# Score products grouped by pass within a PSUM bank, and background VectorE work queued behind a slot's key scaling

## The chip, the cores and the metric

The kernel runs on one core of one Trainium2 chip. The metric is the device time of one execution in microseconds; where several executions were timed, the median is given.

## The reference, cut to what matters

A block of three parts adds to x (512 tokens in 8 groups of 64, width 512): a cross-attention part that also holds a self-attention, a sparse attention part, and a feed-forward part with ternary weights. Most of the time goes into the cross-attention over the context, which has 1601 rows for each of the 8 groups:

```python
kvx = jnp.einsum('bsi,oi->bso', cond, w_kv_x)
kx, vx = jnp.split(kvx, 2, axis=-1)
kx = _ln(kx.reshape(b, sc, g, d), kxln_w, kxln_b)      # g = 8 heads of d = 128
scores = jnp.einsum('bsghd,btgd->bghst', q, k) * scale
p = jax.nn.softmax(scores, axis=-1)
return jnp.einsum('bghst,btgd->bsghd', p, v)
```

The matrix products are wanted at float32 accuracy. The kernel therefore splits each operand into a high and a low part and adds three products: high by high, high by low, low by high.

## The kernel before, in words

**Foreground.** The 1601 context rows of a group are cut into 13 tiles of 128 (the last has 65). One loop runs over 208 slots, one for each tile of each of 16 `Cross` objects (8 groups by 2 halves of 4 heads each). A tile passes through these steps, each some slots after the one before:

- `keys` (L515 to L538): load, split into `cThi` and `cTlo` (ScalarE, GpSimd), twelve 512-wide matmuls into a PSUM bank `kx` (L528), squares on ScalarE (`sq`, L533), their sum on VectorE (`kxv`, L534), two small GpSimd operations that end with the reciprocal root `rqk` (L535, L173), and the scaling of the keys by it on VectorE (`kn`, L537). That last one releases the bank.
- `keys_t` (L540 to L553): four transposes of `kn` into another bank called `kx` (L219), then `kthi` on ScalarE (L550), the difference `kf` on VectorE (L552), and `ktlo` on ScalarE (L553).
- `scores` (L555 to L575), once per chunk of two tiles, or three for the last chunk. The scores of one head are 256 wide (322 in the last chunk). [...] Each head is three matmuls (L571 to L573) and one reduction on VectorE (L574), which copies the scores to the SBUF tile `S`, and whose accumulator is read out into the running maxima `cmx`.
- `probs_t`, `context`, `weigh`, 16 slots later: transposes of the exponentials `S` into a bank `pt` (L593), its split into `phi` and `plo`, and twelve 512-wide matmuls into four accumulator banks (L620 to L622).

**Banks.** After slot 15 the pool `pm` of three banks serves all of `kx` (both uses), `s`, `pt`, `xo` and `xt`. A bank's next matmul waits until the last reader of the bank's previous content is done.

**Background.** Projections, self-attention, the sparse attention and the making of ternary weights are Python generators in three streams, `bgA`, `bgB` and `bgC`. At the end of each slot the loop pumps some steps out of them (L1130 to L1137). For `bgB` the pump stands in `tc.issue_after(paced[0].ins)`, where `paced[0]` is the slot's load of context rows: instructions of the same engine as that load (the queue of SP) are queued behind it.

**Order.** The instructions are not queued in the order in which they are written. A scheduler orders each engine's queue when the program is built, using its own model of time; every engine then runs its queue strictly in that order. `tc.issue_after(x)` is a constraint for this scheduler: what the block adds on the engine of `x` stands behind `x` in that engine's queue. It adds no wait between engines.

Of the kernel before, what the change touches and what calls it, by code (L numbers as in the profile page):

```python
# [4 lines left out]

# [12 lines left out]
ALU = mybir.AluOpType  # L18
# [3 lines left out]
P = 128  # L22
# [4 lines left out]
D = 128  # L27
NH = 16
G = 8
HG = 4  # L30
# [7 lines left out]
NCH = len(CHUNKS)  # L38
# [19 lines left out]
def tile_perceiver(ctx: ExitStack, tc: tile.TileContext, t: dict):  # L58
    nc = tc.nc
    V, A, GP, PE = nc.vector, nc.scalar, nc.gpsimd, nc.tensor  # L60
# [16 lines left out]
    def nm(s):  # L77
        uid[0] += 1
        return f"{s}_{uid[0]}"

    def ctile(shape, dt, tag):
        return const.tile(shape, dt, tag=tag, name=tag)

    def sm(tag, k=1, dt=F32, bufs=None):
        kw = {} if bufs is None else {"bufs": bufs}
        return small.tile([P, k], dt, tag=tag, name=nm(tag), **kw)
# [5 lines left out]
    def mainp(tag="m"):  # L92
        return pm.tile([P, 512], F32, tag="m", name=nm(tag))

    def kxp(tag="kx"):


        if lane["late"] is not None:
            return lane["late"]
        return accp(tag) if lane["wide"] else mainp(tag)  # L100
# [35 lines left out]
    def v3(ap, g):  # L136
        return ap.rearrange("p (g k) -> p g k", g=g)
# [4 lines left out]
    class Late:  # L142
# [13 lines left out]
        ps = staticmethod(lambda tag="b": kxp())  # L156
# [68 lines left out]
    zeros = ctile([P, 1], F32, "zeros")  # L225
# [264 lines left out]
        return hi, lo  # L490

    paced = [None]

    class Cross:

# [19 lines left out]
        def keys(self, tt):  # L515

            t0, n = TT[tt]
            raw = mp.tile([P, NIC, P], F32, tag="raw", name=nm("cTr"), bufs=3)
            paced[0] = nc.sync.dma_start(raw[:, :, :n], t["ctxT"][self.b].rearrange("(c p) k -> p c k", p=P)[:, :, t0:t0 + n])
            chi = mp.tile([P, NIC, P], F32R, tag="cThi", name=nm("cThi"), bufs=2)  # L520
            clo = mp.tile([P, NIC, P], F32R, tag="cTlo", name=nm("cTlo"), bufs=2)
            A.copy(chi[:, :, :n], raw[:, :, :n])  # L522
            GP.tensor_tensor(clo[:, :, :n], raw[:, :, :n], chi[:, :, :n].bitcast(F32), ALU.subtract)  # L523
            ps = kxp()
            k = 0
            for st, mv in ((chi, self.wk[0]), (chi, self.wk[1]), (clo, self.wk[0])):
                for ic in range(NIC):
                    PE.matmul(ps[:n], lhsT=st[:, ic, :n], rhs=mv[:, ic, :], start=k == 0, stop=k == 11)  # L528
                    k += 1
            kn = mp.tile([P, 512], F32, tag="kn", name=nm("kn"), bufs=3)  # L530
            sq = mp.tile([P, 512], F32, tag="sq", name=nm("sq"), bufs=1)
            v = sm("kxv", HG)
            A.activation(sq[:n], ps[:n], AF.Square, scale=1.0 / math.sqrt(D))  # L533
            V.tensor_reduce(v[:n], v3(sq[:n], HG), AX.X, ALU.add)  # L534
            GP.tensor_scalar(v[:n], v[:n], EPS, None, ALU.add)  # L535
            r = rsqrt(v[:n], n, HG, "rqk")
            V.tensor_tensor(v3(kn[:n], HG), v3(ps[:n], HG), r.unsqueeze(2).to_broadcast([n, HG, D]), ALU.mult)  # L537
            self.kn[tt] = kn  # L538

        def keys_t(self, tt):  # L540
# [14 lines left out]
        def scores(self, ci):  # L555
            chunk = CHUNKS[ci]
            cw = sum(TT[tt][1] for tt in chunk)
            hi, lo = self.kt.pop(ci)
            N = cw + (cw & 1)
            if N > cw:  # L560
                GP.memset(hi[:, :, cw:N].bitcast(F32), 0.0)
                GP.memset(lo[:, :, cw:N].bitcast(F32), 0.0)
            sc = mp.tile([P, HG, KTW], F32, tag="S", name=nm("S"), bufs=7)
            self.S[ci] = sc
            per = 512 // N
            for g in range(HG):
                if g % per == 0:
                    bank = mainp("s")
                ps = bank[:, g % per * N:(g % per + 1) * N]
                q = slice(g * P, (g + 1) * P)  # L570
                PE.matmul(ps, lhsT=self.qhi[:, q], rhs=hi[:, g, :N], start=True, stop=False)  # L571
                PE.matmul(ps, lhsT=self.qhi[:, q], rhs=lo[:, g, :N], start=False, stop=False)
                PE.matmul(ps, lhsT=self.qlo[:, q], rhs=hi[:, g, :N], start=False, stop=True)  # L573
                V.tensor_tensor_reduce(sc[:, g, :cw], ps[:, :cw], zeros.to_broadcast([P, cw]), 1.0, -3.0e38,  # L574
                                       ALU.add, ALU.max, self.mx[:, g * NCH + ci:g * NCH + ci + 1])  # L575

        def maxima(self):
            self.nmx = sm("cnm", HG)
# [467 lines left out]
    bgB = Stream()  # L1046
# [4 lines left out]
    for g in range(NA + LAG + 3):  # L1051
        nA, kA = divmod(g, NT)
        if g < NA and kA == 0:
            h = work[nA].half
            if h not in wk:
                wk[h] = key_weights(h)
            work[nA].wk = wk[h]
        if g == LAG - 1:
            lane["wide"] = False
        if g == NA + 3:  # L1060
            lane["late"] = mainp("late")
        e = g - LAG + 1
        if 0 <= e < NA:
            nE, kE = divmod(e, NT)
            w = work[nE]
            w.context(kE)
            w.probs_t(kE)
            ci = CHUNK_OF[kE]
            if ci + 1 < NCH:

                with tc.issue_after(w.pin.ins):
                    w.exps(ci + 1, *((0, 2) if kE == CHUNKS[ci][0] else (2, 4)))
        if g < NA:
            work[nA].keys(kA)
        if g == 0:
            bgA.pump(ALL)
        if g == 2:
            bgA.add(norms(rest), projection("qx", range(4), rest), projection("qx", range(4, 8), range(NJ)),
                    projection("q", range(8), range(NJ)), projection("k", range(4), range(NJ)), projection("v", range(4), range(NJ)))
            bgA.add(*[self_attn(j) for j in range(NJ)])  # L1080
            bgA.add(attn_consts())
        if g == TERNARY_AT:
            bgB.add(ternary("ffn_w1", w1t), ternary("ffn_w2", w2t))
        if 0 <= g - 2 < NA:
            nS, kS = divmod(g - 2, NT)
            ci = CHUNK_OF[kS]
            w = work[nS]
            if kS == CHUNKS[ci][-1]:
                if ci == 0:
                    w.queries()  # L1090
                w.scores(ci)
                if ci == NCH - 1:
                    w.maxima()
                    w.exps(0, 0, 2)
        if 0 <= g - 3 < NA and (g - 3) % NT == NT - 1:
            work[(g - 3) // NT].exps(0, 2, 4)
        e = g - LAG
        if 1 <= e and e % NT == 0 and e // NT <= len(work):
            work[e // NT - 1].values()
        if 2 <= e and (e - 1) % NT == 0 and (e - 1) // NT <= len(work):  # L1100
            w = work[(e - 1) // NT - 1]
            key = (w.b // 2, w.half)
            j, odd = divmod(w.b, 2)
            split = w.half and j >= NJ - SPLIT
            if not odd:
                bgA.clear_front()
                if w.half:
                    bgA.pump(ALL)
                catq[key] = cat_tile("catx")
            w.cat(catq[key])  # L1110
            if key != (NJ - 1, 1):
                if not w.half:
                    if odd:
                        bgA.front.append(proj_part(j, 16, catq[key]))
                elif split or odd:
                    on = (odd * S, S) if split else (0, P)
                    bgA.add(finish(j, 24, catq[key], *on))
            elif not odd:
                bgC.add(proj_weights(24), finish(NJ - 1, 24, catq[key], 0, S, True, Late()))
            else:  # L1120
                bgA.add(finish(NJ - 1, 24, catq[key], S, S, True))
        if 0 <= e < NA:
            nE, kE = divmod(e, NT)
            work[nE].weigh(kE)
            if kE == NT - 1:
                work[nE].weighed()
        if 0 <= g - 1 < NA:
            nT, kT = divmod(g - 1, NT)
            work[nT].keys_t(kT)
        for bg, q in ((bgA, PACE[g >= LATER]), (bgC, PACE[1]), (bgB, TERNARY_PACE if g < NA + FFN_AT else 0)):  # L1130
            n = int((g + 1) * q) - int(g * q)
            if bg is bgB:

                with tc.issue_after(paced[0].ins):
                    bg.pump(n)
            else:
                bg.pump(n)  # L1137
        if g == NA + FFN_AT:
            bgB.pump(ALL)
            if NJ > 2:  # L1140
                bgB.add(ffn(list(range(NJ - 2)), 0))
                bgB.step()
# [74 lines left out]
```

## Time and profile before

| what | value |
|---|---|
| median of 3 runs | 2084.85 us (2074.91 to 2086.65) |
| the profiled execution | 2083.31 us |
| its span, first to last instruction | 2081.6 us |
| mean granted TensorE clock | 0.988 |
| TensorE matmuls busy | 1979.7 us, 10923 records |
| VectorE, ScalarE, GpSimd busy | 1390.4, 1304.4, 952.9 us |
| DMA | 257.34 MB, mean 124 GB/s |
| last score matmul starts | 1885.4 us |

A busy time of matmuls is not their work: the matmuls overlap, and their ends are modelled. In the timeline, 512-wide matmuls that follow each other without a wait start about 0.23 us apart, 256-wide ones 0.12 us, 128-wide ones 0.11 us, while the record of one lasts 0.39, 0.28 and 0.27 us. Idle time of TensorE is thus the time in which not even a tail of a record is left. In the list of waits each line gives the waiting instruction, what released it, the total in us, the number of times, and the longest.

### The profile page before, as it was taken

How to read it: one execution, taken by the hardware profiler on the slowest of the kernel's cores; microseconds unless marked ns; L12 is line 12 of the kernel's file. 1: busy time of each engine (PE TensorE's matmuls, PEld its weight loads, DVE VectorE, ACT ScalarE, POOL GpSimd, SP SyncE). 2: the span in 40 equal slices, each digit the busy share in tenths (PEclk: the TensorE clock that was granted, in tenths of full speed). 3: DMA queues.
4: the chain of work that ended last, by engine and by line, in shares of the span. 5: the costliest groups of instructions: out<-in, count | busy, mean ns of one | idle time of the engine just before them, and what ended most of it. 6: DMA issues, size and time to landing. Idle time of an engine off the chain costs nothing. (4 is left out here: it accounts for less than half of the span.)

```text
span 2081.6 us, 32709 instructions
## 1 busy us (share of the span) xinstructions
PE 1979.7 (95%) x10923; PEld 1633.8 (78%) x10923; DVE 1390.4 (67%) x3344; ACT 1304.4 (63%) x2787; POOL 952.9 (46%) x1018
## 2 busy tenths in 40 slices
PE   5889999999999899999999999999999999999998
PEld 4778878888778788887888888787878778877776
DVE  7876676576676775767777777675755665576665
ACT  5666757677666666665656656666556665566554
POOL 5454545454454444445444544444454445542232
PEclk9999999999999999999999999999999999999999
DMA  5443343444334444544544454432433223333325
GB/s 180 127 116 112 113 124 110 122 135 127 107 117 130 140 144 123 173 133 156 161 142 148 142 176 145 142 106 69 127 104 109 77 77 97 87 93 101 114 69 170
DMA packets 261817, 257.34 MB, mean 124 GB/s; under 512 B 25408, under 2 KB 186304, under 8 KB 261648
## 3 DMA queue, kind: packets, MB, share of 16 engines
q1 hardware_dynamic: 261648, 255.25, 41.1%
q8 instruction: 86, 1.41, 0.3%
q14 instruction: 83, 0.68, 0.1%
HBM read 231.33 MB, written 23.59 MB: 122 GB/s over the span
## 5 line engine op out<-in xcount | busy, mean ns | idle before, releaser
L523 POOL TENSOR_TENSOR cTlo<-cTr,cThi 128x512 fp32r<-128x512 f32 (+1 forms) x208 | 267.6, 1286 | 497.7 <-ACT cThi L522 352.5
L607 POOL TENSOR_TENSOR clo<-cr,chi 128x512 fp32r<-128x512 f32 (+1 forms) x208 | 277.2, 1333 | 292.8 <-ACT chi L606 273.3
L621 PE MATMUL acc<-plo,chi 128*128 128x512 f32 (+1 forms) x832 | 336.0, 405 | 1.5 <-DVE plo L597 1.5
L622 PE MATMUL acc<-phi,clo 128*128 128x512 f32 (+1 forms) x832 | 327.0, 395 | 0.0
L534 DVE TENSOR_REDUCE kxv<-sq 128x4 f32<-128x512 f32 (+1 forms) x208 | 141.9, 682 | 237.3 <-ACT sq L533 236.7
L620 PE MATMUL acc<-phi,chi 128*128 128x512 f32 (+1 forms) x832 | 254.5, 405 | 5.6 <-ACT phi L596 2.9
L528 PE MATMUL kx<-wkhi,cThi 128*128 128x512 f32 (+1 forms) x832 | 242.9, 413 | 13.0 <-DVE kf L552 4.0
L550 ACT ACTIVATE kthi<-kx,cols 128x512 fp32r<-128x512 f32 (+1 forms) x208 | 159.0, 764 | 145.6 <-PE kx L219 144.7
L606 ACT CAST chi<-cr 128x512 fp32r<-128x512 f32 (+1 forms) x208 | 128.4, 617 | 166.9 <-PE acc L621 117.1
L528 PE MATMUL kx<-wklo,cThi 128*128 128x512 f32 (+1 forms) x832 | 229.4, 398 | 0.0
L173 POOL TENSOR_TENSOR rqk<-kxv,mhalf 128x4 f32<-128x4 f32 (+1 forms) x208 | 219.0, 1053 | 17.2
L528 PE MATMUL kx<-wkhi,cTlo 128*128 128x512 f32 (+1 forms) x832 | 225.7, 393 | 0.0
L522 ACT CAST cThi<-cTr 128x512 fp32r<-128x512 f32 (+1 forms) x208 | 125.2, 602 | 126.8 <-PE kx L528 59.9
L574 DVE CUSTOM_DVE_ANT_0 S<-s,zeros 128x256 f32<-128x256 f32 (+1 forms) x384 | 157.1, 429 | 64.4 <-PE s L573 63.2
L584 ACT ACTIVATE S<-S,cnm 128x256 f32<-128x256 f32 (+1 forms) x384 | 196.4, 518 | 1.8 <-DVE cnm L579 1.8
L528 PEld LDWEIGHTS kx<-wklo,cThi 128*128 128x128 f32 (+1 forms) x832 | 155.8, 187 | 40.9 <-POOL wklo L489 0.5
L528 PEld LDWEIGHTS kx<-wkhi,cThi 128*128 128x128 f32 (+1 forms) x832 | 146.8, 188 | 50.1 <-DVE cmx L574 6.8
L620 PEld LDWEIGHTS acc<-phi,chi 128*128 128x128 f32 (+1 forms) x832 | 151.5, 189 | 42.8 <-ACT phi L596 5.8
L552 DVE SCALAR_TENSOR_TENSOR kf<-kx,cols,kthi 128x512 f32<-128x512 f32 (+1 forms) x208 | 150.8, 725 | 49.9 <-ACT kthi L550 49.0
L528 PEld LDWEIGHTS kx<-wkhi,cTlo 128*128 128x128 f32 (+1 forms) x832 | 153.9, 185 | 38.2
L537 DVE TENSOR_TENSOR kn<-kx,rqk 128x512 f32<-128x512 f32 (+1 forms) x208 | 142.5, 685 | 59.0 <-POOL rqk L173 57.9
L621 PEld LDWEIGHTS acc<-plo,chi 128*128 128x128 f32 (+1 forms) x832 | 157.0, 189 | 29.1 <-DVE plo L597 2.2
(320 smaller groups left out, 4120.2 us busy)
## 6 DMA issues: line engine op xcount, KB each, us to landing
cTr<-in_ctxT SPq DMA_DIRECT2D x192, 256.0 KB
cr<-in_ctx SPq DMA_DIRECT2D x192, 256.0 KB
ld<-in_wproj SPq DMA_DIRECT2D x128, 256.0 KB
wv<-in_wkv SPq DMA_DIRECT2D x64, 256.0 KB
tern<-in_ffn_w SPq DMA_DIRECT2D x64, 256.0 KB
wb<-w1t SPq DMA_DIRECT2D x24, 256.0 KB
wb<-w2t SPq DMA_DIRECT2D x24, 256.0 KB
ld<-lnTd SPq DMA_DIRECT2D x19, 256.0 KB
```

The lines of the kernel that those rows point to most:

```text
L173: GP.tensor_tensor(y[:n], v, mhalf[:n, :k], ALU.pow)
L523: GP.tensor_tensor(clo[:, :, :n], raw[:, :, :n], chi[:, :, :n].bitcast(F32), ALU.subtract)
L528: PE.matmul(ps[:n], lhsT=st[:, ic, :n], rhs=mv[:, ic, :], start=k == 0, stop=k == 11)
L537: V.tensor_tensor(v3(kn[:n], HG), v3(ps[:n], HG), r.unsqueeze(2).to_broadcast([n, HG, D]), ALU.mult)
L550: A.activation(hi[:, :, o], v3(pt, HG)[:, :, :n], AF.Identity, bias=hb["kx"], scale=hw["kx"])
L552: V.scalar_tensor_tensor(kf[:, :, :n], v3(pt, HG)[:, :, :n], hw["kx"], hi[:, :, o].bitcast(F32), ALU.mult, ALU.subtract)
L574: V.tensor_tensor_reduce(sc[:, g, :cw], ps[:, :cw], zeros.to_broadcast([P, cw]), 1.0, -3.0e38, ALU.add, ALU.max, self.mx[:, g * NCH + ci:g ...
L584: A.activation(self.S[ci][:, g, :cw], self.S[ci][:, g, :cw], AF.Exp, bias=self.nmx[:, g:g + 1], accum_out=self.su[:, g * NCH + ci:g * NCH ...
L607: GP.tensor_tensor(clo[:n], raw[:n], chi[:n].bitcast(F32), ALU.subtract)
L620: PE.matmul(self.U[ic], lhsT=chi[:n, s], rhs=phi[:n], start=tt == 0, stop=False)
L621: PE.matmul(self.U[ic], lhsT=chi[:n, s], rhs=plo[:n], start=False, stop=False)
L622: PE.matmul(self.U[ic], lhsT=clo[:n, s], rhs=phi[:n], start=False, stop=last)
```

## The change

Two things change. In `scores`, the matmuls of all heads in a bank are issued pass by pass: first high by high for each head, then low query by high key, and last high query by low key. Only the first matmul into the bank carries the start flag. The reductions of the bank's heads follow after all of its matmuls. In the main loop, all three background streams are pumped in `tc.issue_after(pin[0].ins)`, where `pin[0]` is the newest scaling of keys (`kn`), a VectorE instruction; `bgB` keeps its other constraint.

```diff
+    pin = [None]
...
-            V.tensor_tensor(v3(kn[:n], HG), v3(ps[:n], HG), r.unsqueeze(2).to_broadcast([n, HG, D]), ALU.mult)
+            pin[0] = V.tensor_tensor(v3(kn[:n], HG), v3(ps[:n], HG), r.unsqueeze(2).to_broadcast([n, HG, D]), ALU.mult)
...
             per = 512 // N
-            for g in range(HG):
-                if g % per == 0:
-                    bank = mainp("s")
-                ps = bank[:, g % per * N:(g % per + 1) * N]
-                q = slice(g * P, (g + 1) * P)
-                PE.matmul(ps, lhsT=self.qhi[:, q], rhs=hi[:, g, :N], start=True, stop=False)
-                PE.matmul(ps, lhsT=self.qhi[:, q], rhs=lo[:, g, :N], start=False, stop=False)
-                PE.matmul(ps, lhsT=self.qlo[:, q], rhs=hi[:, g, :N], start=False, stop=True)
-                V.tensor_tensor_reduce(sc[:, g, :cw], ps[:, :cw], zeros.to_broadcast([P, cw]), 1.0, -3.0e38,
-                                       ALU.add, ALU.max, self.mx[:, g * NCH + ci:g * NCH + ci + 1])
+            for g0 in range(0, HG, per):
+                bank = mainp("s")
+                gs = range(g0, g0 + per)
+
+                for k, (a, x) in enumerate(((self.qhi, hi), (self.qlo, hi), (self.qhi, lo))):
+                    for i, g in enumerate(gs):
+                        PE.matmul(bank[:, i * N:(i + 1) * N], lhsT=a[:, g * P:(g + 1) * P], rhs=x[:, g, :N],
+                                  start=k == 0 and i == 0, stop=k == 2, skip_group_check=True)
+                for i, g in enumerate(gs):
+                    ps = bank[:, i * N:(i + 1) * N]
+                    V.tensor_tensor_reduce(sc[:, g, :cw], ps[:, :cw], zeros.to_broadcast([P, cw]), 1.0, -3.0e38,
+                                           ALU.add, ALU.max, self.mx[:, g * NCH + ci:g * NCH + ci + 1])
...
-            if bg is bgB:
-
-                with tc.issue_after(paced[0].ins):
-                    bg.pump(n)
-            else:
+
+            with tc.issue_after(pin[0].ins), tc.issue_after(paced[0].ins) if bg is bgB else nullcontext():
                 bg.pump(n)
```

More of the change, by code (lines that the diff above doesn't have):

```diff
@@ L2 @@
 from collections import deque
-from contextlib import ExitStack
+from contextlib import ExitStack, nullcontext
 from types import SimpleNamespace
```

## The prediction

> **What bounds the kernel now.** I read the page first: TensorE is busy in 95% of the span and in eight or nine tenths of nearly every slice, VectorE in 67%.
>
> ```profile
> span 2081.6 us, 32709 instructions
> ...
> PE 1979.7 (95%) x10923; PEld 1633.8 (78%) x10923; DVE 1390.4 (67%) x3344; ACT 1304.4 (63%) x2787; POOL 952.9 (46%) x1018
> ...
> PE   5889999999999899999999999999999999999998
> ```
>
> So TensorE's queue sets the end. An edit pays only if it shortens TensorE's work, which it doesn't (same matmuls, same sizes), or its waits. The list of TensorE's waits is therefore the second view:
>
> ```profile
> PE pt L593 <- DVE cmx L574: 14.0, 16, 1.9
> ...
> PE kx L219 <- DVE kn L537: 10.4, 13, 3.6
> PE kx L219 <- DVE cmx L574: 6.3, 13, 1.5
> PE s L571 <- DVE cmx L574: 6.1, 10, 1.2
> PE pj L328 <- DVE xq L301: 5.7, 1, 5.7
> ...
> PE kx L528 <- DVE cmx L574: 4.0, 9, 1.6
> ```
>
> The reader is to see that four of these lines name one releaser, the score reduction L574: 14.0 + 6.3 + 6.1 + 4.0 = 30.4 us. None of the four waits for a score as data (the exponentials stand between). They wait for a bank which L574 was the last to read. The third view, the timeline of TensorE and then VectorE at one such wait, shows why L574 is late:
>
> ```profile
> 134.66 0.39 PE L571 MATMUL s<-kthi,qxhi 128*128 128x256 f32 x1 [0.24 <-DVE cmx L574]
> 134.89 0.28 PE L572 MATMUL s<-ktlo,qxhi 128*128 128x256 f32 x1
> 135.01 0.28 PE L573 MATMUL s<-kthi,qxlo 128*128 128x256 f32 x1
> 135.13 0.28 PE L571 MATMUL s<-kthi,qxhi 128*128 128x256 f32 x1
> 135.25 0.29 PE L572 MATMUL s<-ktlo,qxhi 128*128 128x256 f32 x1
> 135.37 0.28 PE L573 MATMUL s<-kthi,qxlo 128*128 128x256 f32 x1
> 137.24 0.80 PE L593 MATMUL pt<-ident,S 128*128 128x128 f32 x4 [1.59 <-DVE cmx L574]
> ```
>
> ```profile
> 134.52 0.42 DVE L574 CUSTOM_DVE_ANT_0 S<-s,zeros 128x256 f32<-128x256 f32 x1
> 134.87 0.08 DVE L574 DVE_READ_ACCUMULATOR2_ANT cmx<- 128x1 f32 x1
> 135.39 1.25 DVE L350 TENSOR_SCALAR hrs<-rq,cols 128x4 f32<-128x4 f32 x1 [0.44 <-POOL rq L173]
> 136.68 0.16 DVE L352 SCALAR_TENSOR_TENSOR hnb<-hag,hrs 128x4 f32<-128x4 f32 x1
> 136.76 0.42 DVE L574 CUSTOM_DVE_ANT_0 S<-s,zeros 128x256 f32<-128x256 f32 x1
> ```
>
> Two banks are filled here. TensorE wrote each bank's first head, waited 0.24 us at 134.66 until VectorE had read it, and then wrote the second heads. The next user of a bank, `pt`, follows at once and stands 1.59 us, because the reduction of the second head is queued behind `hrs`, a background instruction that itself waits for GpSimd.
>
> **What the Trainium skill says.** "PSUM — Partial Sum Buffer", section "PSUM bank collisions raise a hardware error", says that two engines must not touch one bank (in one group of 32 partitions) at once, and that PSUM is to be guarded by bank and not by address. The trace agrees: at 134.66 a matmul into the free half of a bank waits for the reduction of the other half. In the same page, "Engine vs sequencer instructions", VectorE's queue is strict first in, first out and matmuls keep program order. The two timelines agree: the reduction that TensorE needs stays behind `hrs`, and nothing overtakes the waiting `pt`. "The four PSUM rules" says a start flag clears the written marks of the whole bank, hence one flag per bank in the change. No run yet shows that.
>
> **The change, part by part.**
>
> *Scores.* In the program as built before, a two-head bank goes TensorE, VectorE, TensorE, VectorE. In the changed one it goes six matmuls, then two reductions. There are 16 x 5 x 2 = 160 such banks; the last chunk's 64 one-head banks only change the order of their products. So 160 waits of TensorE disappear as instructions: in the two built programs all waits of matmuls fall from 2884 to 2727. What this is worth I read from the built orders, laying matmuls end to end at the trace's pace (0.23, 0.15, 0.12 and 0.11 us for 512, 322, 256 and 128 columns). Of the 160 banks, the next matmul into the same bank stands on average 1.55 us of matmuls behind the bank's last score matmul before, and 3.26 us after. It stands less than 1.5 us behind it 132 times before and 13 times after. A bank is being filled for 3.54 us before and 1.39 us after. The release needs two L574 at most (0.43 + 0.08, less overlap: about 0.35 each) plus what stands in VectorE's queue. From the last score matmul to the end of the bank's last L574, this trace has a mean of 1.3 us, with a tenth above 2.5. After the change both reductions follow the last matmul, so I add one, 0.35 us: about 1.65, against a spacing of 3.26. Of the 30.4 us, 26.1 are released by L574 of width 256 (the timeline's forms), which is what this part can reach; 4.3 us belong to one-head banks, whose spacing stays (below 1.5 us 27 and 24 times). Scaling the 26.1 by 13/132 leaves 2.6: **23.5 us saved**. Bounds: nothing, if the waits only change their name; 30 if the tails below the idle count vanish too.
>
> *Low key product last.* TensorE waits for `ktlo` 0.2 us in the whole list. Worth nothing. The queries' low part, now second, is made once per 13 slots, long before.
>
> *Pin.* No DMA, GpSimd or ScalarE instruction is bound by it: it acts on VectorE alone. In the built orders some 380 background instructions on VectorE move from ahead of their slot's `kn` to behind it. Yet earlier slots' background still stands there: the VectorE work between `kxv` and `kn` is 1.21 us per slot before and 1.27 after, under GpSimd's round trip of about 1.6 us. So `kn` isn't nearer. All TensorE waits released by `kn` come to 12.2 us; I take 0 saved, with bounds of 12 saved and, for background that comes late, 33 lost (second rival).
>
> *Start.* The pin reorders the first 30 us visibly. Before, two norms (L191 0.68 and 0.65 us, two L193 0.17, two L195 0.14; 1.5 us net of overlap) and three more L319 (0.4 us each net, 1.2) stand ahead of `xq` L301, for which TensorE idles 5.7 us with no other work. After, they stand behind it. **2.7 us saved**; the norms themselves come later under key matmuls, and cost nothing unless the projections that read their rows come to wait for them.
>
> *Given back.* When TensorE runs earlier, the next latest releaser is met: `kn` (12.2 us in all), `kf` (4.0), the splits. Spread over the same slots, I let them take 4 us. What hides VectorE's work is TensorE's own; VectorE is at 67%, and moves by one point.
>
> Sum: 23.5 + 2.7 - 4 = 22 us. Against the profiled execution, 2083.3 - 22 = 2061; this execution lies 1.5 us under the median of the runs, so against the median **2062 us**.
>
> **Rivals.**
>
> 1. *Given back entirely* (within 10 us of before, about 2082). The bank wait is only where VectorE's lateness becomes visible; a late queue would show at `kn`, `kf` or `plo` instead. For: in the timeline above it is a background instruction that is late. Against: these three have far more room. The first transpose of `kn` stands 10.4 us of matmuls behind the keys' last matmul in both orders, `plo`'s first use 5.3 and 5.6 us behind its transposes. The bank of scores was the one tight place.
>
> 2. *Background late on VectorE, slower.* Queued behind `kn`, a background chain loses most of a slot at each link, while TensorE's queue has its background matmuls at fixed places; each late one stops the foreground behind it. Place: projections and output products, some 300 groups of matmuls (`pj`, `pp`, `po`, `tr`, `p2`). Apart from the start, TensorE waits about 13 us for such producers now (`ws`, `fa`, `xq` and the like), 0.04 us per group. It decides once it adds more than the 22 us saved, 0.07 us per group; if it adds 33, 0.11 us per group, the time is 2095. For: 380 instructions moved, and the scheduler's model of time isn't the chip. Against: it also delays the background matmuls accordingly (the last projection product stands 17 us of matmuls later in the new order, the last output product 2 us), and the tail after the last slot is as long as before.
>
> 3. *More than forecast*: the `kn` waits go too, and the unfilled time under the tails of records. 30 + 12 + 3 = 45 us, 2040.
>
> **How the numbers follow.** A difference below about 0.5%, 10 us, can't be told from none here. Forecast, 12 to 36 us saved: 0.58. Rival 3: 0.09. Rival 1: 0.14. Rival 2: 0.19. Faster is 0.58 + 0.09 = 0.67 (nearly all of these pass 10 us), same 0.14, slower 0.19. The likeliest case's own range is 2049 to 2073. The range for 8 in 10 reaches from rival 3's 2036 (its 45 us plus a spread of 4) to 2094, which takes in rival 1 and the nearer half of rival 2.
>
> **What would show it.** Right: the four L574 lines fall from 30.4 to under 8 us in sum, second-head waits are gone, VectorE's own wait for L573 (two per bank before) shrinks, and TensorE's first idle before `pj` is about 3 us. Wrong: L574 stays above 20 us; or `kn`, `kf`, `hst`, `ws`, `fa` grow as releasers of TensorE by as much as L574 loses; or the slices after 40 us are no denser.

## The result, and the profile after

| | before | changed |
|---|---|---|
| median of 8 runs | 2085.36 us (2074.91 to 2089.58) | 2070.18 us (2066.94 to 2074.93) |
| profiled execution's span | 2081.6 us | 2068.5 us |

The ratio is 0.9931, with a 95% interval of 0.9915 to 0.9947: 14.4 us faster at 2085, where 22 were forecast. TensorE is still busy in 95% of the span, so it still sets the end. Its mean granted clock was 0.988 in the profiled execution before and 0.987 in the one after, so the gain isn't the clock's. The page's head:

```profile
span 2068.5 us, 32686 instructions
...
PE 1970.6 (95%) x10923; PEld 1630.2 (79%) x10923; DVE 1394.3 (67%) x3344; ACT 1300.9 (63%) x2787; POOL 960.4 (46%) x1018
```

The same 10923 matmul records fill 9.1 us less busy time, and TensorE's idle time falls by only 4.0 us. Since the work and the clock are the same, the 9.1 us must have been waits too: short ones, hidden under the modelled tails of the matmuls before them (the last section counts them). The list of TensorE's waits shows where the rest moved. First two lines of before that the prediction doesn't show, then the list after. Its longest wait, 12.3 us for `fa` (11.4 before), stands almost wholly in the start:

```profile
...
PE kx L528 <- DVE kf L552: 4.0, 6, 1.5
...
PE acc L620 <- ACT phi L596: 2.9, 4, 1.2
```

```profile
...
PE kx L529 <- DVE kf L553: 11.8, 13, 1.8
PE pt L596 <- DVE cmx L577: 8.4, 13, 1.5
PE acc L623 <- ACT phi L599: 5.4, 8, 1.5
PE pj L328 <- ACT ws L318: 4.9, 2, 4.5
PE pj L328 <- DVE xq L301: 4.0, 1, 4.0
...
PE kx L529 <- DVE cmx L577: 2.7, 7, 1.1
...
PE kx L219 <- DVE cmx L577: 2.0, 3, 1.1
...
PE kx L529 <- DVE kn L538: 2.0, 2, 1.4
```

The score reduction (now L577) released TensorE after 30.4 us of idling before, and after 13.1 us now. The scaling `kn` falls from 12.5 us (all its lines) to 3.9. In their place stand `kf`, from 4.0 to 11.8 us, `phi`, from 2.9 to 5.6, and one wait of 4.5 us for `ws`, where it was 1.25.

The timeline of the changed kernel shows a pair of score banks at about the time of the excerpt in the prediction (two heads of 256 columns share a bank, `per = 512 // N` in the diff), TensorE and then VectorE:

```profile
132.81 0.64 PE L573 MATMUL s<-ktlo,qxhi 128*128 128x256 f32 x4
133.29 2.08 PE L328 MATMUL pj<-ws,xq 128*128 128x256 f32 x16
135.21 0.60 PE L219 MATMUL kx<-ident,kn 128*128 128x128 f32 x4
135.65 0.60 PE L596 MATMUL pt<-ident,S 128*128 128x128 f32 x4
```

```profile
133.25 0.42 DVE L577 CUSTOM_DVE_ANT_0 S<-s,zeros 128x256 f32<-128x256 f32 x1 [1.63 <-PE s L573]
...
133.60 0.42 DVE L577 CUSTOM_DVE_ANT_0 S<-s,zeros 128x256 f32<-128x256 f32 x1
...
133.94 0.42 DVE L577 CUSTOM_DVE_ANT_0 S<-s,zeros 128x256 f32<-128x256 f32 x1
...
134.28 0.42 DVE L577 CUSTOM_DVE_ANT_0 S<-s,zeros 128x256 f32<-128x256 f32 x1
```

Both banks' low key products end together, and four reductions follow in one run. The next users of the pool's banks, the transposes at 135.21 and 135.65, come 1.9 us or more after the end of the last score matmul (0.12 us after its start) and don't wait. Nothing alternates any more.

Measured bank by bank over the whole trace, from the records of the score matmuls and reductions (a matmul counts as ended 0.12 us after its start; which of two interleaved banks a record belongs to is inferred from the order):

| two-head banks, mean us | before | changed |
|---|---|---|
| start of the first to end of the last score matmul | 3.98 | 1.54 |
| end of the last score matmul to end of the last reduction | 1.19 | 1.71 |
| bank held, in all | 5.17 | 3.24 |

**Where along the run.** The first key matmul of tile n starts at these times, in one profiled execution of each kernel (us from the span's start):

| tile | before | scores alone | constraint alone | whole change |
|---|---|---|---|---|
| 10 | 87.9 | 91.3 | 85.9 | 88.8 |
| 50 | 438.1 | 439.1 | 435.2 | 431.8 |
| 75 | 678.3 | 670.1 | 672.3 | 664.6 |
| 100 | 915.5 | 908.6 | 903.3 | 899.9 |
| 207 | 1864.6 | 1858.3 | 1863.1 | 1848.8 |
| end of span | 2081.6 | 2077.6 | 2086.4 | 2068.5 |

Most of the gain, 13.7 of 15.8 us, is there by tile 75, while the projections run as background (`pj` until 829 us), and is then kept. At tile 10 nothing is gained yet. The tail after tile 207 gives 2.7 us back.

### The profile page after: what moved, and what is told of

The parts are those of the page before. It is cut to its first block, busy times and chain, and to the rows that moved or that the text cites. A ratio compares the mean times of both kernels' runs of the same rounds, so it can differ in the third digit from the quotient of the medians.

```text
span 2068.5 us, 32686 instructions
## 1 busy us (share of the span) xinstructions
PE 1970.6 (95%) x10923; PEld 1630.2 (79%) x10923; DVE 1394.3 (67%) x3344; ACT 1300.9 (63%) x2787; POOL 960.4 (46%) x1018
## 5 line engine op out<-in xcount | busy, mean ns | idle before, releaser
L529 PE MATMUL kx<-wkhi,cThi 128*128 128x512 f32 (+1 forms) x832 | 243.7, 414 | 21.6 <-DVE kf L553 11.8
L623 PE MATMUL acc<-phi,chi 128*128 128x512 f32 (+1 forms) x832 | 247.5, 403 | 9.4 <-ACT phi L599 5.4
L625 PEld LDWEIGHTS acc<-phi,clo 128*128 128x128 f32 (+1 forms) x832 | 157.3, 189 | 27.8 <-issue 0.8
```

Source lines behind the costliest of these rows:

```text
L623: PE.matmul(self.U[ic], lhsT=chi[:n, s], rhs=phi[:n], start=tt == 0, stop=False)
L625: PE.matmul(self.U[ic], lhsT=clo[:n, s], rhs=phi[:n], start=False, stop=last)
```

## The experiments

Theory A is that of the prediction: the two turns of a bank between TensorE and VectorE are the cost, and the constraint is worth little. Theory B: the constraint on VectorE is what pays. Theory C: a schedule drawn anew moves the time by this much, whatever the edit. All ratios are to the kernel before, run on the same chip between the variants.

### The two halves

Scores alone: the whole change, less its constraint.

```diff
-            with tc.issue_after(pin[0].ins), tc.issue_after(paced[0].ins) if bg is bgB else nullcontext():
+            with tc.issue_after(paced[0].ins) if bg is bgB else nullcontext():
```

> The scores part alone (pass by pass within the bank, reductions after all of a bank's matmuls), without the new VectorE constraint. Theory A (the bank's two turns between TensorE and VectorE were the cost, the constraint gives little): at least three quarters of the 14.4 us of the whole change, so a ratio of 0.991 to 0.995 to the kernel before; TensorE's waits on the score reduction fall from 30.4 us to 8 to 15. Theory B (the constraint gives most of it): a ratio of 0.997 to 1.001. Theory C (the two need each other, or any new draw of the schedule moves the time by this much): no prediction beyond 0.990 to 1.005.

Measured: 0.9978 (0.9965 to 0.9991), 22 runs. TensorE's waits on the reduction fall to 16.1 us, just above the 8 to 15 that A has; but the time gains a third of the whole change and not three quarters. By the time alone it is B's case. `kn` stays at 10.7 us, so it isn't the spacing of banks that takes these waits away.

The constraint alone: the changed kernel with the `scores` of before.

> The VectorE constraint alone, with the scores as before (a head at a time, each with its reduction). Theory A: a ratio of 0.997 to 1.001 to the kernel before, of which about 0.0013 is the start (xq 1.7 us earlier); TensorE's waits on the score reduction stay at 25 to 35 us. Theory B: 0.992 to 0.995. The waits on kn, which fell from 12.2 to 3.9 us with the whole change, should fall here too if the constraint did that, and should not if the spacing of banks did.

Measured: 1.0012 (1.0002 to 1.0023), 22 runs. No gain: B, which wanted 0.992 to 0.995, is out. But the waits on `kn` do fall to 3.6 us, so the constraint does its own part. What it gives back is seen in this kernel's list of waits:

```profile
PE s L572 <- DVE cmx L575: 11.0, 13, 4.1
...
PE acc L621 <- ACT phi L597: 9.9, 10, 1.6
```

The first line is the second head of a bank waiting for the first head's reduction: 11.0 us, where it was 6.1. `phi` takes 9.9 us, where it was 2.9.

The halves add up to -0.0010 and the whole is -0.0069. So they seem to help each other, though the difference of 0.006 is not far above what a new draw of the schedule moves, and a part of it is the clock (both below). The delay of `kn` fits this reading. From the records of all 208 tiles (us; `kn` is timed from the start of the tile's last key matmul to its own end):

| | before | scores alone | constraint alone | whole |
|---|---|---|---|---|
| `rqk` ready to start of `kn`, mean | 0.38 | 0.45 | 0.28 | 0.37 |
| tiles with over 1 us there | 21 | 35 | 11 | 22 |
| tiles with `kn` over 7 us after their last key matmul | 17 | 21 | 13 | 7 |
| VectorE between `rqk` ready and `kn`, us over all tiles: score reductions | 10.1 | 29.1 | 12.2 | 28.2 |
| the same: everything else | 70.5 | 69.4 | 47.3 | 54.0 |

The grouped scores put bunches of two to four reductions on VectorE, and some 19 us more of them stand ahead of `kn`. The constraint takes 15 to 23 us of other work out of its way. Alone, it meets banks that still need VectorE twice.

### Inside the bank

Head by head within the bank, in the old product order, but with both reductions after all six matmuls and without the constraint:

```diff
-                for k, (a, x) in enumerate(((self.qhi, hi), (self.qlo, hi), (self.qhi, lo))):
-                    for i, g in enumerate(gs):
+                for i, g in enumerate(gs):
+                    for k, (a, x) in enumerate(((self.qhi, hi), (self.qhi, lo), (self.qlo, hi))):
```

> As scores_only, but inside a bank head by head (three products of one head, in the old order high by high, high by low, low by high, then three of the next), with both reductions still after all six matmuls; no VectorE constraint. Theory A says that only the reductions' place matters: within 0.002 of scores_only. If the low product's place last or the pass by pass order matters, it is slower than scores_only by over 0.003.

Measured: 1.0001 (0.9988 to 1.0014), 14 runs, 0.0023 above scores alone: between the two expectations. The waits on the reduction are 17.6 us, nearly the 16.1 of the pass by pass form. From the first to the last score matmul a bank takes 2.17 us here, and 1.48 there, so the order does count for how long a bank is filled.

Only the order of products, with the reductions where they were:

```diff
-                PE.matmul(ps, lhsT=self.qhi[:, q], rhs=lo[:, g, :N], start=False, stop=False)
-                PE.matmul(ps, lhsT=self.qlo[:, q], rhs=hi[:, g, :N], start=False, stop=True)
+                PE.matmul(ps, lhsT=self.qlo[:, q], rhs=hi[:, g, :N], start=False, stop=False)
+                PE.matmul(ps, lhsT=self.qhi[:, q], rhs=lo[:, g, :N], start=False, stop=True)
```

> Only the order of the three products is changed (high by high, low query, low key last), head by head, each head with its own reduction, no VectorE constraint. If the order of products is worth nothing, as I put it in the prediction: within 0.0015 of the kernel before. If it is why the pass by pass form (0.9978) was faster than the head by head form in the old product order (1.0001): 0.996 to 0.999. TensorE's waits on the score reduction stay near 30 us either way.

Measured: 1.0020 (1.0003 to 1.0038), 13 runs. No gain, as the prediction had it; that it is slower lies inside the scatter that comes next. TensorE's waits on the reduction were 25.4 us here, so they scatter too.

### How much a new order moves the time

Neither edit, only the background's pace, 1.61 steps per slot before:

```diff
-PACE = 1.61, 4
+PACE = 1.60, 4
```

> The kernel before with the background's pace at 1.60 steps per slot instead of 1.61: a control. Neither edit of the change is in it; the scheduler only gets a slightly shifted background and draws another order. If a mere new draw of the order moves the time little, it is within 0.0015 of the kernel before; if the differences between the variants (0.9931 for the whole change, 0.9978 and 1.0012 for its parts) are draws, it moves by 0.003 or more.

> The same control with 1.62 steps per slot. Together with the other one it gives the scatter of draws; same expectation.

Measured: 1.0027 (1.0015 to 1.0039), 16 runs, at 1.60, and 1.0046 (1.0030 to 1.0061), 6 runs, at 1.62. So a shift of the background by less than 1% moves the time by 6 to 10 us with much the same waits (33.1 and 30.0 us on the reduction). Theory C holds for differences of 0.003 to 0.005: neither half of the change, nor the order inside the bank, can be ranked by its time alone. Is the whole change then a draw as well? The change at both paces:

> The whole change with the background's pace at 1.60. The kernel before at this pace came to 1.0027 of the kernel before at 1.61. If the change's gain is a property of its two edits, this lies 10 to 20 us under that: a ratio of 0.993 to 0.998 to the kernel before at 1.61. If the gain at 1.61 was mostly a lucky draw of the order, it is at 1.000 to 1.005.

> The whole change at pace 1.62; the kernel before at this pace came to 1.0046. Gain from the edits: 0.995 to 1.000. A lucky draw at 1.61: 1.002 to 1.007.

| pace | before | changed | changed to before | waits on reduction, `kn`, `kf`, before | the same, changed |
|---|---|---|---|---|---|
| 1.61 | 1 | 0.9931 | 0.9931 | 30.4, 12.5, 4.0 us | 13.1, 3.9, 11.8 us |
| 1.60 | 1.0027 | 0.9884 (0.9864 to 0.9903), 4 runs | 0.986 | 33.1, 14.1, 4.3 us | 13.2, 2.9, 10.2 us |
| 1.62 | 1.0046 | 0.9959 (0.9946 to 0.9973), 9 runs | 0.991 | 30.0, 13.8, 5.2 us | 17.0, 3.4, 14.1 us |

The fourth column is the quotient of two ratios from different chips, so good to about 0.003. The gain is there in all three draws: 0.7, 1.4 and 0.9%, on average 1.0% or 21 us. The redistribution of the waits repeats as well: the reduction and `kn` fall, `kf` rises. So theory C alone doesn't explain the whole change; it can account for the spread between 0.7 and 1.4%. The gain at 1.60 is larger than the 10 to 20 us that were expected.

Part of the draws is the clock. Each run lists TensorE's mean granted clock. Among the runs of one kernel it goes with the time: over 244 runs, a clock lower by 0.001 goes with 1.4 us more (correlation -0.80 within kernels). The means of the kernels differ too:

| kernel | mean granted clock of its runs |
|---|---|
| before, on three chips | 0.9875 to 0.9879 |
| whole change at 1.61, 1.60, 1.62 | 0.9875, 0.9872, 0.9863 |
| scores alone; constraint alone | 0.9848; 0.9852 |
| before at 1.60; at 1.62 | 0.9858; 0.9853 |
| wider constraint below, new scores; old scores | 0.9878; 0.9808 |

At 1.4 us per 0.001, an estimate from these runs, the clock makes up 2 of the 6 us at pace 1.60, 3 of the 10 at 1.62, and about 4 us in each half. At an equal clock the scores alone would gain some 9 us, over half of the whole, the constraint alone 1, and the halves would fall short of the whole by some 4 us and not 12. The gain of the whole change is not the clock's, or hardly: its clock at 1.60 and 1.62 is above that of the kernel before at the same pace by 0.001, some 2 us of 29 and 19. No run holds the clock fixed; what comes before a fall of it is shown in the last section.

### The start

The constraint in slots 0 to 7 alone, with the new scores:

```diff
-            with tc.issue_after(pin[0].ins), tc.issue_after(paced[0].ins) if bg is bgB else nullcontext():
+            with tc.issue_after(pin[0].ins) if g < 8 else nullcontext(), tc.issue_after(paced[0].ins) if bg is bgB else nullcontext():
```

> The whole change, but the VectorE constraint only in slots 0 to 7. Theory A with the constraint's worth in the start alone: within 0.002 of the whole change (0.993), and 1 to 3 us under scores_only. If the constraint is worth something in the steady state, it lies 4 us or more above the whole change; if it costs something there, below it.

Measured: 0.9958 (0.9941 to 0.9976), 11 runs: between scores alone (0.9978) and the whole (0.9931), 5.6 us above the whole. As expected beforehand for a worth in the steady state, though 5.6 us is no more than what the controls moved. The start itself is better read from the trace. The changed kernel gains 1.7 us at `xq` (5.7 to 4.0) and loses it again 45 us later:

```profile
70.21 0.58 PE L328 MATMUL pj<-ws,xq 128*128 128x256 f32 x1 [4.52 <-ACT ws L318]
```

ScalarE makes `ws` only at 69.65, when it has waited 4.75 us for that projection's weights:

```profile
69.65 0.91 ACT L318 ACTIVATE ws<-ld,cols 128x256 fp32r<-128x256 f32 x2 [4.75 <-DMA ld<-in_wqx]
```

In the changed kernel's built order (the order of the queues) that load stands in SP's queue behind the stores and loads of the norms, and these come later because their VectorE instructions stand behind `kn`. Before, the wait at this place was 1.25 us. Without the constraint the wait is 1.4 us at most, in all six kernels that lack it. With it, seven of eight kernels wait 3.5 to 4.6 us here, at all three paces and with old scores (3.5) as with new; only the constraint alone has no such wait of TensorE, though ScalarE waits 3.8 us for the weights there as well. So it comes with the constraint and isn't a draw. That the norms hold up the load was read from the queue and not isolated.

### A wider constraint

With the change, `kf` and the reduction lead the waits. So the background was queued also behind the newest `kf`, score reduction and `plo`:

```diff
-            with tc.issue_after(pin[0].ins), tc.issue_after(paced[0].ins) if bg is bgB else nullcontext():
+            pins["kf"] = V.scalar_tensor_tensor(kf[:, :, :n], v3(pt, HG)[:, :, :n], hw["kx"], hi[:, :, o].bitcast(F32), ALU.mult, ALU.subtract)
...
+                    pins["s"] = V.tensor_tensor_reduce(sc[:, g, :cw], ps[:, :cw], zeros.to_broadcast([P, cw]), 1.0, -3.0e38,
...
+            pins["plo"] = V.tensor_tensor(lo[:n], pt[:n], hi[:n].bitcast(F32), ALU.subtract)
...
+            with ExitStack() as st:
+                for x in (pin[0], *pins.values(), *([paced[0]] if bg is bgB else [])):
+                    st.enter_context(tc.issue_after(x.ins))
                 bg.pump(n)
```

> The whole change, with the background on VectorE queued also behind the newest kf, score reduction and plo of the loop, not behind kn alone. With the whole change kf became the second releaser of TensorE (11.8 us, 4.0 before) and 13.1 us stay with the score reduction. If background work ahead of these on VectorE is the cause, those two fall to 15 us in sum and the ratio to before is 0.986 to 0.991. If they wait for their own inputs, or background late on VectorE holds TensorE instead, it is no better than the whole change: 0.993 or above.

Measured: 0.9871 (0.9848 to 0.9894), 6 runs, median 2057.12 us: some 12 us under the whole change. Its waits:

```profile
PE kx L530 <- DVE kf L554: 10.1, 11, 1.8
PE pt L597 <- DVE cmx L578: 5.5, 10, 1.4
PE acc L624 <- ACT phi L600: 5.1, 7, 1.3
```

The reduction falls from 13.1 to 9.5 us in all, `kf` hardly, from 11.8 to 10.8. Their sum is 20.3 and not 15: the time came as expected, its explanation only in part. The rest is spread: all idle time on the list is 80.7 us, where it was 92.7, and TensorE's busy time falls by another 4.6 us, to 1966.0. The time is a single draw, and on another chip than the whole change.

The same with the scores of before:

> The wider constraint (background on VectorE behind the newest kn, kf, score reduction and plo), but with the scores a head at a time as before. With both it was 0.9871. If the constraint works by itself: 0.988 to 0.993. If the bank's two turns between TensorE and VectorE must go first, as the kn constraint alone (1.0012) suggests: 0.996 or above, with 25 us or more of TensorE's waits on the score reduction.

Measured: 1.0051 (1.0031 to 1.0070), 8 runs. With the wider constraint, old scores and new are 0.018 apart, four times a draw; by the estimate above some 0.005 of it is the clock. The waits on the reduction fall to 17.0 us all the same, below the 25 that were expected, and still the time doesn't follow: TensorE's busy time rises to 1987.8 us, by 8.1 over before. The lower clock makes up about 10 of the 11 us that this kernel lies above before, so by that estimate the wider constraint with the old scores is worth about nothing, and not less. The list of waits, which counts idle time alone, shows neither this nor the short waits.

The same constraint on ScalarE too (background there also behind `sq`, `kthi`, `ktlo` and `phi`, each set like this one):

```diff
-            A.activation(sq[:n], ps[:n], AF.Square, scale=1.0 / math.sqrt(D))
+            pins["sq"] = A.activation(sq[:n], ps[:n], AF.Square, scale=1.0 / math.sqrt(D))
```

> The wider constraint with the new scores, and the same for ScalarE: background there also behind the newest sq, kthi, ktlo and phi. TensorE still waits for kf 10.8 us (VectorE waits for kthi before it) and for phi 5.1 us. If background on ScalarE is ahead of these, the two halve and the ratio to before is 0.981 to 0.986; if late background on ScalarE holds TensorE instead, 0.987 or above.

Measured: 0.9863 (0.9840 to 0.9887), 5 runs: no different from the wider constraint on VectorE alone. `kf` falls to 7.1 us, `phi` rises to 6.6, and `ws` rises from 4.8 to 10.2. It looks as if late background on ScalarE takes what the foreground gains; with one draw this isn't shown.

## Why the prediction was right or wrong

- **What bounds the kernel, and the mechanism: right.** The bank of scores was the tight place. Two reductions after six matmuls hold it for 3.24 us and not 5.17, and the waits on the reduction fell in each of three draws, by 43 to 60%. Of the signs that were named, the waits on second heads are gone, and VectorE's own waits for the last score product fell from 63.2 to 33.8 us. The four lines came to 13.1 us, neither under 8 nor above 20.
- **Scores, 23.5 us: too large.** The waits of TensorE on reductions of width 256 were 26.1 us and are 10.7, so 15.4 came off. The term that failed is the scaling "by 13/132". It counts banks whose next user stands less than 1.5 us behind. But the release itself has a median of 1.52 us after the change and a tenth of them above 2.7 us, so a bank with 2 us of room still waits. Counted as in the prediction, from the start of the last matmul, the release has a mean of 1.83 us where 1.65 was estimated and 1.31 was measured before. The threshold should have moved with it: in the built order after, 32 banks have under 2 us of room and 58 under 2.5. 26.1 x 58/132 is 11.5 us, close to the 10.7 measured.
- **Low key product last, nothing: right** as far as its own run can tell (1.0020, within the scatter).
- **Pin, nothing: right for the constraint alone (1.0012), wrong in its reason.** I compared means: the VectorE work between `kxv` and `kn`. The mean delay is indeed the same, 0.38 and 0.37 us. But TensorE waits only for outliers, and tiles with `kn` over 7 us after their matmuls fell from 17 to 7; the waits on `kn` lost 8.6 us (the full list before has 12.5, a little more than the 12.2 of the prediction). And I did not see that the grouped reductions would delay `kn` by themselves, so that the constraint may be worth more with them than without.
- **Start, 2.7 us saved: wrong.** 1.7 us came, and 3.3 us went (4.5 against 1.25) at the place that the prediction named but did not price, the projections. That these wait because of the late norms was read from the queue.
- **Given back, 4 us: too small.** `kf` alone rose by 7.8 us, and `phi` by 2.7. As for `kf`: the next user of a bank of transposed keys is often the next tile's key matmul (98 banks before, 88 after), 3.6 us of matmuls behind in the built orders, and `kf` has to be done by then. It ended later than that after the last transpose in 26 tiles before and in 37 after.
- **Rivals.** The second, late background on VectorE, shows at most in the 3.3 us at the start, a tenth of its price of 33 us; the slight loss of the constraint alone is no more than its clock explains. The first took part: of 26 us that the reduction and `kn` lost, 10 went to `kf` and `phi`.
- **The size.** 14.4 us against 22 forecast. Three draws of the schedule gave 0.7, 1.4 and 0.9%, so the forecast of 1.1% hit their mean better than each term of its sum deserved. That is luck in part: the scores were put 8.1 us too high, `kn` 8.6 too low, what is given back at least 6.5 too low. And the sum took a wait off the idle list as time off the run, while idle time fell by 4.0 us only and most of the gain came from waits too short to be on the list.

## What to carry to other kernels

Where two engines must take turns on a bank, do all of the writer's work in it, then all of the reader's. Here that took the time for which a bank is held from 5.17 to 3.24 us. A constraint on an engine's queue is worth trying together with the change that creates the need for it, and not only alone: here neither half by itself was worth more than 0.3%, and together they gave 0.7 to 1.4%, though how much of that is interplay isn't settled. When a scheduler draws the order, measure what a neutral shift does (here 0.3 to 0.5%) and compare the granted clocks before reading anything into smaller differences.

## What the runs showed of the hardware that had not been expected

**TensorE's idle time isn't its lost time.** Waits shorter than the tail of the matmul before them appear as busy time. The distance from one matmul's start to the next shows them. Where it exceeds the median for the matmul's width by more than 0.02 us, the excess adds up to 221 us before and 203 us after the change: a difference of 18 us, where idle time shows 4. Sorted by the matmul that starts late (us, one execution each):

| | before | scores alone | constraint alone | whole |
|---|---|---|---|---|
| `pt` (transposes of `S`) | 31.6 | 18.5 | 20.2 | 15.7 |
| transposes of `kn` | 24.3 | 20.3 | 15.3 | 6.2 |
| scores | 18.8 | 9.8 | 22.8 | 12.9 |
| keys | 31.6 | 44.2 | 34.8 | 43.5 |
| any, at half clock (see below) | 22.4 | 25.2 | 26.8 | 21.4 |
| all others | 92.0 | 94.9 | 107.0 | 103.3 |

The users of the scores' banks and of `kn` lose 40 us less with the whole change, and the keys, which wait for `kf`, 12 us more.

**Behind a wait, the clock is often lower.** The traces record stretches in which TensorE is granted half its clock, 3.4 to 17.1 us long: 49.6 us in all before, 52.2 us after. In them the 512-wide matmuls start 0.43 us apart and not 0.23. The end of one, which lasts from 128.7 to 132.2 us, is seen in the changed kernel's timeline:

```profile
131.64 0.63 PE L624 MATMUL acc<-plo,chi 128*128 128x512 f32 x1
132.07 0.44 PE L625 MATMUL acc<-phi,clo 128*128 128x512 f32 x1
132.35 0.39 PE L624 MATMUL acc<-plo,chi 128*128 128x512 f32 x1
132.58 0.40 PE L625 MATMUL acc<-phi,clo 128*128 128x512 f32 x1
```

Of 177 such stretches in the fourteen traces, 149 follow directly on 3.4 us in which the matmuls, at the median distances, would fill less than half the time. Counted the other way, between 40 and 1950 us: after 98 of 170 such windows at full clock half clock followed, after fuller ones in 10 of 7519. The wait of 1.59 us in the prediction's timeline is one case: half clock follows from 137.6 to 141.0 us. The wider constraint with the old scores has 75.9 us at half clock. Outside these stretches its excess is 192 us, against 198 us before: it is slower in them alone. That the waits bring the lower clock about is read from this order of events; no run isolates it.
